# Experts' tiles in pairs while there are two, and the odd last one as a job of its own, in a graph, attention and expert layer on Trainium2

## The chip, the cores and the metric

The kernel runs on one core of a Trainium2 chip. The metric is the device time of one execution in microseconds; less is better. TensorE (PE) multiplies matrices, with its weight loads shown apart (PEld), VectorE (DVE) and ScalarE (ACT) do elementwise work, GpSimd (POOL) issues the indirect transfers, and SyncE (SP) the plain ones of this stage.

## The reference

A layer for 6250 tokens of 256 features and 100000 edges. After a layer norm it adds a graph convolution (mean over the neighbours) and a linear attention; both come before the stage that changes here. Then, on the layer norm of that result, each token goes to one of 8 experts, an MLP of 256 to 1024 to 256 with ReLU:

```python
T = B * L                                           # 6250
C = max(1, math.ceil(CAPACITY_FACTOR * T / E))      # 977
probs = jax.nn.softmax(x @ gate_w + gate_b, axis=-1)
idx = jnp.argmax(probs, axis=-1)
prb = jnp.take_along_axis(probs, idx[:, None], axis=1)[:, 0]
pos = (jnp.cumsum(one_hot, axis=0) * one_hot).sum(-1).astype(jnp.int32) - 1
kept = pos < C
buf = jnp.zeros((E, C, D), dtype=h.dtype).at[idx, pos_safe].set(x, mode='drop')
hmid = jax.nn.relu(jnp.einsum('ecd,edf->ecf', buf, w1) + b1[:, None, :])
ybuf = jnp.einsum('ecf,efd->ecd', hmid, w2) + b2[:, None, :]
y_tok = ybuf[idx, pos_g] * (prb * kept)[:, None]
y = jnp.nan_to_num(y, nan=0.0, posinf=10000.0, neginf=-10000.0)
```

The result is the sum of the layer's input to this stage and y. A token beyond an expert's 977 places gets no expert's output. Everything is in f32.

## The kernel before

The work runs in three stretches. The first normalises the tokens, sorts the edges and prepares the attention. The second, the gather stage, goes over 49 blocks of 128 tokens and multiplies gathered neighbour rows (tile zb) and rows kept in SBUF (z_s) with matrices of counts in add_rows (L821, L822). Beside it, in groups of up to 7 blocks, gate_pieces normalises finished tokens, picks their expert, writes a row of 513 numbers for each (normalised token, residual, probability) to buf_d in device memory, and adds to the tile places, which holds, for each of 64 tiles of 128 places (8 experts, 8 tiles each), which token stands there (L1091). ebase holds the running numbers of tokens of each expert (L1044).

The third stretch, from L1160 on, is the expert stage. It begins with a table worked out on VectorE, replicated over the partitions. From the number of tokens of each expert, capped at CAP = 977, it makes the number of pairs of tiles of each expert (a shift by 8 bits, L1173), their running sum cum (seven additions of one column, L1177), for each of NS = 32 numbers of a pair its expert exp_f and its place among that expert's pairs, and from these the column of places of each of its two tiles. One matmul (L1198) picks these columns out of places, transposed, and its output is cast into idx_s (L1199), the rows of buf_d to gather, and tki_s (L1204), the rows of the output to store. exp_s (L1205, L1206) holds the experts' numbers and the number of pairs, to be read into registers.

Then come the pairs, each 256 places of one expert, whether its second tile holds tokens or not. A pair s goes through four steps:

- fetch(s): SP reads the experts' numbers into registers, four at a time, and loads the expert's weights with expert_weights (L854): w1e and w2e of 1 MB each and two biases, in tiles of three buffers. POOL gathers the pair's two tiles of 128 rows into bt (L1222), four buffers.
- turned(s): four transposes on PE into pB (L1230), and one copy to bT on VectorE (L1232).
- up(s): for each of 8 blocks f of 128 hidden features two matmuls of 256 columns into pu (L1241; three buffers), and an activation with bias and ReLU into hm on ACT (L1242).
- down(s): for each of the two tiles 8 matmuls of 256 columns into pd (L1250; two buffers), then eight VectorE instructions (L1253 to L1263), which add the bias, multiply by the probability, limit what is not finite and add the residual, and an indirect store by POOL (L1264).

The loop runs over S0 = 24 pairs, with fetch three pairs ahead and turned and up one pair ahead of down:

```python
for s in range(S0):
    if s + 3 < S0:
        fetch(s + 3)
    if s + 1 < S0:
        turned(s + 1)
        up(s + 1)
    down(s)
```

Pairs beyond the 24th lie in blocks of rest, under branches on the number of pairs that is read at the end: two, then more, each pair's four steps one behind the other. The order of instructions on each engine is that of a scheduler, which keeps to the data's order; PE runs, as compiled, the transposes of the next pair, the first two matmuls of down of this one, all of up of the next pair, and the remaining fourteen of down of this one. Waits are semaphores, set by the framework for each tile.

Of the kernel before, what the change touches and what calls it, by code (L numbers as in the profile page):

```python
# [7 lines left out]
F32 = mybir.dt.float32  # L8
BF16 = mybir.dt.bfloat16
F32R = mybir.dt.float32r  # L10
I32 = mybir.dt.int32
AF = mybir.ActivationFunctionType
OP = mybir.AluOpType
AX = mybir.AxisListType
ET = mybir.EngineType

P = 128
N = 6250
D = 256
NT = 49  # L20
# [45 lines left out]
NE, F = 8, 1024  # L66
FC = F // P
CAP = 977
ET_ = -(-CAP // P)
SP_ = ET_ // 2  # L70
NS = 32
S0 = 24
EPS = 1e-5
NZ = 19
OWN = 0.4
# [10 lines left out]
def gnn_mix_moe_kernel(ctx: ExitStack, tc: tile.TileContext, x, src, dst, w1t, b1g, w2t, b2g,  # L86
                       kw, kb, vw, vb, gate_w, gate_b, fw1, fb1, fw2, fb2, out):
    nc = tc.nc
# [10 lines left out]
    const = ctx.enter_context(tc.tile_pool(name="const", bufs=1))  # L99
# [16 lines left out]
    lane = const.tile([P, P], F32, name="lane")  # L116
# [13 lines left out]
    cj = const.tile([P, 2], F32, name="cj")  # L130
    for j in range(2):
        nc.vector.tensor_scalar(cj[:, j:j + 1], prow, -float(j), None, op0=OP.add)
    idx_s = const.tile([P, 2 * NS], I32, name="idx_s")
    tki_s = const.tile([P, 2 * NS], I32, name="tki_s")
    exp_s = const.tile([1, NS + 1], I32, name="exp_s")
    eps = const.tile([P, 1], F32, name="eps")
    nc.vector.memset(eps, EPS)

# [16 lines left out]
    bias = const.tile([P, D], F32, name="bias")  # L155
# [20 lines left out]
    with tc.tile_pool(name="early", bufs=1) as ep, tc.tile_pool(name="work", bufs=2) as wp, \  # L176
# [305 lines left out]
        pn, pr, f = None, None, 1.0  # L482
# [42 lines left out]
        for i, (pat, base0) in enumerate((([[1, NB + 1]], 0), ([[0, NB + 1]], SEG // BW))):  # L525
# [7 lines left out]
                                op1=OP.bitwise_or)  # L533
# [181 lines left out]
        for q in range(1, QL + 1):  # L715
# [39 lines left out]
            j = h // 2  # L755
# [405 lines left out]
    with tc.tile_pool(name="table", bufs=1) as tp, tc.tile_pool(name="wgt", bufs=3) as wgt, \  # L1161
# [4 lines left out]
        def row_of(name, n=NE):  # L1166
            return tp.tile([P, n], F32, name=name)

        cnt, cum = row_of("cnt"), row_of("cum")
        nc.vector.tensor_scalar(cnt, ebase[:, NT, :], float(CAP), float(2 * P - 1), op0=OP.min, op1=OP.add)  # L1170
        cni = tp.tile([P, NE], I32, name="cni")
        nc.vector.tensor_copy(cni, cnt)
        nc.vector.tensor_scalar(cni, cni, 8, None, op0=OP.logical_shift_right)  # L1173
        nc.vector.tensor_copy(cum, cni)
        nc.vector.tensor_scalar(cum[:, :1], cum[:, :1], 1.0, None, op0=OP.max)
        for e in range(1, NE):
            nc.vector.tensor_add(cum[:, e:e + 1], cum[:, e:e + 1], cum[:, e - 1:e])  # L1177
        gone = tp.tile([P, NS, NE], F32, name="gone")
        nc.vector.tensor_tensor(gone, cum[:, None, :].to_broadcast([P, NS, NE]),
                                lane[:, :NS, None].to_broadcast([P, NS, NE]), op=OP.is_le)  # L1180
# [5 lines left out]
        nc.vector.scalar_tensor_tensor(col, exp_f, float(SP_), beg, op0=OP.mult, op1=OP.add)  # L1186
        nc.vector.tensor_scalar(col, col, 2.0, None, op0=OP.mult)
        nt = NE * ET_
        pick = tp.tile([P, NS, 2], F32, name="pick")
        nc.vector.tensor_tensor(pick[:nt], col[:nt, :, None].to_broadcast([nt, NS, 2]),  # L1190
                                cj[:nt, None, :].to_broadcast([nt, NS, 2]), op=OP.is_equal)
        plc = tp.tile([P, nt], F32, name="plc")
        nc.vector.scalar_tensor_tensor(plc, places[:, nt:], float(P), places[:, :nt], op0=OP.mult, op1=OP.add)
        pT = pp.tile([P, 2, P], F32, name="pT")
        nc.tensor.transpose(pT[:nt, 0, :], plc, ident)
        plT = tp.tile([P, P], F32, name="plT")
        nc.vector.tensor_copy(plT[:nt], pT[:nt, 0, :])
        nc.tensor.matmul(pT[:, 1, :2 * NS], plT[:nt], pick[:nt].rearrange("p s j -> p (s j)"), start=True, stop=True)  # L1198
        nc.vector.tensor_copy(idx_s, pT[:, 1, :2 * NS])  # L1199
        nc.vector.tensor_scalar(plT[:, :2 * NS], pT[:, 1, :2 * NS], float(P), float(2 * NT * P), op0=OP.is_lt,  # L1200
                                op1=OP.mult)
        nc.vector.scalar_tensor_tensor(plT[:, :2 * NS], pT[:, 1, :2 * NS], -float(P), plT[:, :2 * NS], op0=OP.add,
                                       op1=OP.add)
        nc.vector.tensor_copy(tki_s, plT[:, :2 * NS])  # L1204
        nc.vector.tensor_scalar(exp_s[:, :NS], exp_f[:1, :], float(NE - 1), None, op0=OP.min)  # L1205
        nc.vector.tensor_copy(exp_s[:, NS:], cum[:1, NE - 1:])  # L1206


        bts, bTs, hms, experts = {}, {}, {}, {}

        def fetch(s, n=4):

            if s not in experts:
                _, es = nc.values_load_multi_w_load_instructions(
                    exp_s[0:1, s:s + n], engines=[ET.SP], min_val=0, max_val=NE - 1,
                    skip_runtime_bounds_check_because="the number of an expert")
                experts.update({s + i: e for i, e in enumerate(es)})
            if s:
                weights[s] = expert_weights(wgt, experts[s])
            bts[s] = wp.tile([P, 2, RW], F32, name="bt", bufs=4)  # L1220
            for j in range(2):
                nc.gpsimd.indirect_dma_start(  # L1222
                    out=bts[s][:, j, :], out_offset=None, in_=buf_d,
                    in_offset=bass.IndirectOffsetOnAxis(ap=idx_s[:, 2 * s + j:2 * s + j + 1], axis=0))

        def turned(s):
            pT = pp.tile([P, 2, 2, P], F32, name="pB", bufs=2)
            for j in range(2):
                for c in range(2):
                    nc.tensor.transpose(pT[:, c, j, :], bts[s][:, j, c * P:(c + 1) * P], ident)  # L1230
            bTs[s] = wp.tile([P, 2, 2 * P], F32, name="bT")
            nc.vector.tensor_copy(bTs[s], pT.rearrange("p c j q -> p c (j q)"))  # L1232

        def up(s):
            w1e, _, b1e, _ = weights[s]
            hms[s] = wp.tile([P, FC, 2 * P], F32, name="hm")
            bT = bTs.pop(s)
            for f in range(FC):
                pu = pp.tile([P, 2 * P], F32, name="pu", bufs=3)
                for c in range(2):  # L1240
                    nc.tensor.matmul(pu, w1e[:, c, f * P:(f + 1) * P], bT[:, c, :], start=(c == 0), stop=(c == 1))  # L1241
                nc.scalar.activation(hms[s][:, f, :], pu, AF.Relu, bias=b1e[:, f:f + 1])  # L1242

        def down(s):
            _, w2e, _, b2e = weights.pop(s)
            hm, bt = hms.pop(s), bts.pop(s)
            for j in range(2):
                pd = pp.tile([P, D], F32, name="pd", bufs=2)
                for f in range(FC):
                    nc.tensor.matmul(pd, hm[:, f, j * P:(j + 1) * P], w2e[:, f, :], start=(f == 0), stop=(f == FC - 1))  # L1250

                yt = wp.tile([P, D], F32, name="yt", bufs=3)
                nc.vector.tensor_add(yt, pd, b2e)  # L1253
                nc.vector.tensor_scalar(yt, yt, bt[:, j, RW - 1:RW], None, op0=OP.mult)
                lim = wp.tile([P, D], F32, name="lim", bufs=3)
                low = wp.tile([P, D], F32, name="low")
                ok = wp.tile([P, D], I32, name="ok")
                nc.vector.tensor_scalar(lim, yt, FMAX, 1e4, op0=OP.is_gt, op1=OP.mult)
                nc.vector.tensor_scalar(low, yt, -FMAX, 1e4, op0=OP.is_lt, op1=OP.mult)
                nc.vector.tensor_sub(lim, lim, low)  # L1260
                nc.vector.tensor_scalar(ok, yt, 0.0, 0.0, op0=OP.mult, op1=OP.is_equal)
                nc.vector.copy_predicated(lim, ok, yt)
                nc.vector.tensor_add(lim, lim, bt[:, j, D:2 * D])  # L1263
                st = nc.gpsimd.indirect_dma_start(  # L1264
                    out=out, out_offset=bass.IndirectOffsetOnAxis(ap=tki_s[:, 2 * s + j:2 * s + j + 1], axis=0),
                    in_=lim, in_offset=None, bounds_check=N - 1, oob_is_err=False)
                tc.declare_no_dep(st.ins, group="result", reason="each token has one place")
                tc.add_to_no_dep_group("result", st.ins)

        for s in range(3):  # L1270
            fetch(s)
        turned(0)
        up(0)
        for s in range(S0):
            if s + 3 < S0:
                fetch(s + 3)
            if s + 1 < S0:
                turned(s + 1)
                up(s + 1)
            down(s)  # L1280

        used_s = nc.values_load(exp_s[0:1, NS:], min_val=1, max_val=NS,
                                skip_runtime_bounds_check_because="the number of pairs")

        def rest(s, n):

            with tc.If(used_s > s):
                for i in range(s, s + n):
                    fetch(i, n)
                    turned(i)  # L1290
                    up(i)
                    down(i)
                if s + n < NS:
                    rest(s + n, 2 if n < 4 and s + n + 2 < NS - 2 else NS - s - n)

        rest(S0, 2)


# [36 lines left out]
```

## Time and profile before

| | us |
|---|---|
| median of 3 timed runs | 1396.89 (1394.22 to 1400.62) |
| profiled execution | 1385.61 |
| its span, first to last instruction | 1383.8 |
| PE busy | 1128.7 (82%) |
| VectorE busy | 759.6 (55%) |
| POOL busy | 536.2 (39%) |
| ACT busy | 439.7 (32%) |
| mean granted clock of TensorE | 0.924 |

The page shows one profiled execution, taken by the hardware profiler; its times are in microseconds from the first instruction on, and line numbers are those of the kernel. In a row of a group of instructions the name left of the arrow is what is written, then come what is read, the shapes, the number of instructions after the x, the busy time, the mean duration in ns, and the idle time of the engine just before them with what ended it. A matmul's duration counts the time in the pipeline, so consecutive matmuls overlap, and their spacing is shorter than their duration. The chain of waits follows the work that ended last back from the end, from each step to what released it; its pieces are start, length and work.

In this execution the first up of the expert stage starts at 1027.4 and the last store's instruction at 1377.9.

### The profile page before, as it was taken

The numbers are of one execution on the slowest core, as the hardware profiler recorded it, in microseconds if no ns is written. First come the engines' busy times: TensorE is split into PE (matmuls) and PEld (weight loads), VectorE is DVE, ScalarE is ACT, GpSimd is POOL, SyncE is SP. The second block draws the span as 40 slices with busy tenths as digits, with TensorE's granted clock in tenths as the row PEclk, the third lists the DMA queues.
The fourth block names the chain that finished last, engine by engine and source line by source line (L and its number), as shares of the span: only waits on it lengthen the run. The fifth ranks groups of instructions, "written<-read, shape, count | busy, mean of one in ns | idle before, by whom it ended". The sixth has DMA issues, their size and how long they took to land.

```text
span 1383.8 us, 21039 instructions
## 1 busy us (share of the span) xinstructions
PE 1128.7 (82%) x7471; PEld 1012.2 (73%) x7471; DVE 759.6 (55%) x2197; ACT 439.7 (32%) x960; POOL 536.2 (39%) x586
## 2 busy tenths in 40 slices
PE   0688968637879789879888888888849999999997
PEld 0477757536768779778778778778738888888886
DVE  8999776644644654644654544546523443434434
ACT  0567834302223232233233233233513222232221
POOL 0000002056665565656656656666122222232221
PEclk9999989857999889989889989999969999999999
DMA  8674213256876885966966866867565556566550
GB/s 252 200 237 173 99 48 130 96 184 206 286 223 180 224 255 175 256 224 186 269 210 186 246 195 197 219 211 193 191 233 170 200 200 231 178 215 216 201 189 21
DMA packets 147804, 269.91 MB, mean 195 GB/s; under 512 B 19139, under 2 KB 92557, under 8 KB 147692
## 3 DMA queue, kind: packets, MB, share of 16 engines
q0 software_dynamic: 42048, 134.90, 30.9%
q1 hardware_dynamic: 75431, 105.44, 24.9%
q10 hardware_dynamic: 30213, 28.15, 6.5%
q8 instruction: 61, 1.00, 0.3%
q14 instruction: 51, 0.42, 0.1%
HBM read 217.11 MB, written 52.21 MB: 195 GB/s over the span
## 4 chain that ended last, share of the span: by engine, by line
PE 60%; issue 7%; DMA 4%; DVE 4%; another core or an unknown queue 3%; ACT 1%; POOL 0%; ACTq 0%; SPq 0%; POOLq 0%; DVEq 0%
PE pa L821 14%; PE pa L822 13%; PE pu L1241 12%; PE pd L1250 12%; PE pc L918 6%; DMA buf_d<-row 3%; PE lgr L1006 1%; PE ph L998 1%; ACT cn L921 1%; PE pB L1230 1%; DMA bt<-buf_d,idx_s 1%; DVE on L892 0%; DVE og L898 0%; DMA y<-y_d 0%
## 5 line engine op out<-in xcount | busy, mean ns | idle before, releaser
L908 POOL DMA_INDIRECT zb<-z_d,idx x441 | 425.0, 964 | 265.1 <-issue 97.0
L821 PE MATMUL pa<-z_s,cn 128*128 128x258 f32 x1176 | 346.3, 322 | 12.8 <-issue 12.3
L822 PE MATMUL pa<-z_s,cn 128*128 128x256 f32 x1176 | 316.4, 296 | 10.6 <-issue 10.2
L921 ACT CAST cn<-pc 128x512 fp32r<-128x512 f32 x294 | 171.2, 587 | 437.9 <-PE pc L918 138.3
L821 PEld LDWEIGHTS pa<-z_s,cn 128*128 128x128 f32 x1176 | 241.1, 205 | 16.1 <-issue 15.9
L822 PEld LDWEIGHTS pa<-z_s,cn 128*128 128x128 f32 x1176 | 241.0, 205 | 12.7 <-issue 11.9
L892 DVE TENSOR_TENSOR on<-lane_w,nvl 128x1024 bf16<-128x1024 bf16 x147 | 101.2, 688 | 233.8 <-PE pc L918 109.7
L1242 ACT ACTIVATE hm<-pu,b1e 128x256 f32<-128x256 f32 x192 | 90.9, 473 | 266.0 <-PE pu L1241 235.9
L1250 PE MATMUL pd<-w2e,hm 128*128 128x256 f32 x768 | 173.3, 379 | 0.0
L1241 PE MATMUL pu<-bT,w1e 128*128 128x256 f32 x768 | 172.7, 383 | 0.0
L918 PE MATMUL pc<-od,on 128*128 128x128 bf16 x1176 | 125.5, 232 | 53.9 <-issue 26.0
L1241 PEld LDWEIGHTS pu<-bT,w1e 128*128 128x128 f32 x768 | 145.0, 191 | 26.8 <-issue 7.8
L1250 PEld LDWEIGHTS pd<-w2e,hm 128*128 128x128 f32 x768 | 144.1, 190 | 18.6
L1264 POOL DMA_INDIRECT out_dram<-lim,tki_s x48 | 48.3, 1006 | 254.1 <-DVE lim L1263 245.7
L821 PE MATMUL pa<-zb,og 128*128 128x258 f32 x441 | 130.2, 308 | 9.2 <-issue 8.8
L918 PEld LDWEIGHTS <-on 128*128 128x128 bf16 x1176 | 76.9, 103 | 72.3 <-issue 50.0
L822 PE MATMUL pa<-zb,og 128*128 128x256 f32 x441 | 124.9, 296 | 4.1 <-issue 3.7
L1253 DVE TENSOR_TENSOR yt<-pd,b2e 128x256 f32<-128x256 f32 x48 | 20.4, 425 | 192.7 <-PE pd L1250 192.7
L821 PEld LDWEIGHTS pa<-zb,og 128*128 128x128 f32 x441 | 90.1, 204 | 10.5 <-issue 10.3
L822 PEld LDWEIGHTS pa<-zb,og 128*128 128x128 f32 x441 | 90.1, 204 | 8.0 <-issue 8.0
L587 POOL DMA_INDIRECT kb<-srt_d,bi x5 | 5.2, 1044 | 203.2 <-DVE bi L583 202.0
L419 PE MATMUL pz<-w2s,xTa 128*128 128x256 f32 x196 | 56.8, 412 | 13.7 <-ACT xTa L430 13.1
(382 smaller groups left out, 1497.5 us busy)
## 6 DMA issues: line engine op xcount, KB each, us to landing
w1e<-in_fw_dram SPq DMA_DIRECT2D x24, 1024.0 KB
w2e<-in_fw_dram SPq DMA_DIRECT2D x24, 1024.0 KB
z_d<-zr SPq DMA_DIRECT2D x49, 256.0 KB
buf_d<-row SPq DMA_DIRECT2D x6, 1795.5 KB
zb<-z_d,idx POOLq DMA_INDIRECT x441
ovf_d<-zero ACTq DMA_DIRECT2D x1, 6321.0 KB
ov<-ovf_d SPq DMA_DIRECT2D x49, 129.0 KB
y_d<-xg ACTq DMA_DIRECT2D x7, 896.0 KB
```

The costliest lines, as they stand in the source:

```text
L419: nc.tensor.matmul(pz, xT[:, c, :], w2s[:, c, :], start=(c == 0), stop=(c == 1))
L821: nc.tensor.matmul(ps[:, :AW], lhsT, z[:, D:], start=first, stop=False, skip_group_check=True)
L822: nc.tensor.matmul(ps[:, :D], lhsT, z[:, :D], start=False, stop=last, skip_group_check=True)
L892: nc.vector.tensor_tensor(to[b % 2][:, c, :].rearrange("p c (m j) -> p c m j", j=2), lanes[:, None, :w].to_broadcast([P, n, w, 2]), of.to_ ...
L908: nc.gpsimd.indirect_dma_start(out=zb[asked % NZ].bitcast(F32)[:, :DZ], out_offset=None, in_=z_d, in_offset=bass.IndirectOffsetOnAxis(ap=i ...
L918: nc.tensor.matmul(pc[:, j - j0, :], on[:, j // 2, (j % 2) * P:(j % 2 + 1) * P], od[:, j // 2, :], start=True, stop=True, skip_group_check ...
L921: nc.scalar.copy(cn[:, :n, :], pc[:, :n, :])
L1241: nc.tensor.matmul(pu, w1e[:, c, f * P:(f + 1) * P], bT[:, c, :], start=(c == 0), stop=(c == 1))
L1242: nc.scalar.activation(hms[s][:, f, :], pu, AF.Relu, bias=b1e[:, f:f + 1])
L1250: nc.tensor.matmul(pd, hm[:, f, j * P:(j + 1) * P], w2e[:, f, :], start=(f == 0), stop=(f == FC - 1))
L1253: nc.vector.tensor_add(yt, pd, b2e)
L1264: st = nc.gpsimd.indirect_dma_start(out=out, out_offset=bass.IndirectOffsetOnAxis(ap=tki_s[:, 2 * s + j:2 * s + j + 1], axis=0), in_=lim, ...
```

## The change

An expert's tiles are still taken two at a time while there are two. If their number is odd, the last one is a job of its own, of one tile. The table gets the numbers of tiles by a shift of 7 bits, the pairs by one bit more, odd (whether an expert has an odd tile), and ods_, its running sum; own1, of1, exp1 and col1 give for each of up to 8 odd tiles its expert and its column of places, which go into 8 further columns of pick, idx_s and tki_s and into exp_s. The matmul that picks has 72 columns instead of 64. Three numbers (more) decide at the end whether anything is left.

The loop runs over a list of jobs: S0 = 21 pairs and S1 = 3 odd tiles, the latter behind the 5th, 10th and 15th pair. An odd tile is numbered NS + i; turned, up and down work on as many tiles as tiles_of gives: two transposes, an up of 128 columns, a down of one output. Its weights are loaded as those of a pair. At the end one branch guards two chains of rest blocks, one for further pairs and one for further odd tiles.

```diff
-S0 = 24
+S0 = 21
+S1 = 3
+NC = 2 * NS + NE
...
-        nc.vector.tensor_scalar(cnt, ebase[:, NT, :], float(CAP), float(2 * P - 1), op0=OP.min, op1=OP.add)
+        nc.vector.tensor_scalar(cnt, ebase[:, NT, :], float(CAP), float(P - 1), op0=OP.min, op1=OP.add)
         cni = tp.tile([P, NE], I32, name="cni")
         nc.vector.tensor_copy(cni, cnt)
-        nc.vector.tensor_scalar(cni, cni, 8, None, op0=OP.logical_shift_right)
+        nc.vector.tensor_scalar(cni, cni, 7, None, op0=OP.logical_shift_right)
+        nc.vector.tensor_copy(cnt, cni)
+        nc.vector.tensor_scalar(cni, cni, 1, None, op0=OP.logical_shift_right)
         nc.vector.tensor_copy(cum, cni)
         nc.vector.tensor_scalar(cum[:, :1], cum[:, :1], 1.0, None, op0=OP.max)
+        odd, ods_ = row_of("odd"), row_of("ods_")
+        nc.vector.scalar_tensor_tensor(odd, cum, -2.0, cnt, op0=OP.mult, op1=OP.add)
+        nc.vector.tensor_scalar(odd, odd, 0.0, None, op0=OP.max)
+        nc.vector.memset(ods_[:, :1], 0.0)
         for e in range(1, NE):
             nc.vector.tensor_add(cum[:, e:e + 1], cum[:, e:e + 1], cum[:, e - 1:e])
+            nc.vector.tensor_add(ods_[:, e:e + 1], ods_[:, e - 1:e], odd[:, e - 1:e])
...
+        sing = [P, NE, NE]
+        own1, of1 = (tp.tile(sing, F32, name=n) for n in ("own1", "of1"))
+        nc.vector.tensor_tensor(own1, ods_[:, None, :].to_broadcast(sing),
+                                lane[:, :NE, None].to_broadcast(sing), op=OP.is_equal)
+        nc.vector.tensor_mul(own1, own1, odd[:, None, :].to_broadcast(sing))
+        exp1, col1, of_e = row_of("exp1"), row_of("col1"), row_of("of_e")
+        nc.vector.tensor_mul(of1, own1, lane[:, None, :NE].to_broadcast(sing))
+        nc.vector.tensor_reduce(exp1, of1, AX.X, OP.add)
+        nc.vector.scalar_tensor_tensor(of_e, lane[:, :NE], float(ET_), cnt, op0=OP.mult, op1=OP.add)
+        nc.vector.tensor_scalar(of_e, of_e, -1001.0, None, op0=OP.add)
+        nc.vector.tensor_mul(of1, own1, of_e[:, None, :].to_broadcast(sing))
+        nc.vector.tensor_reduce(col1, of1, AX.X, OP.add)
+        nc.vector.tensor_scalar(col1, col1, 1000.0, None, op0=OP.add)
+        nc.vector.tensor_scalar(pick[:nt, 2 * NS:], col1[:nt], cj[:nt, :1], None, op0=OP.is_equal)
...
-        nc.vector.tensor_copy(exp_s[:, NS:], cum[:1, NE - 1:])
+        nc.vector.tensor_copy(exp_s[:, NS:NS + NE], exp1[:1])
+        nc.vector.tensor_add(ods_[:, NE - 1:], ods_[:, NE - 1:], odd[:, NE - 1:])
+        more = row_of("more", 3)
...
+        nc.vector.tensor_copy(exp_s[:, NS + NE:], more[:1])
...
+        def tiles_of(s):
+            return (2 * s, 2 * s + 1) if s < NS else (NS + s,)
...
         def up(s):
             w1e, _, b1e, _ = weights[s]
+            q = P * len(tiles_of(s))
             hms[s] = wp.tile([P, FC, 2 * P], F32, name="hm")
             bT = bTs.pop(s)
             for f in range(FC):
-                pu = pp.tile([P, 2 * P], F32, name="pu", bufs=3)
+                pu = pp.tile([P, 2 * P], F32, name="pu", bufs=3)[:, :q]
                 for c in range(2):
-                    nc.tensor.matmul(pu, w1e[:, c, f * P:(f + 1) * P], bT[:, c, :], start=(c == 0), stop=(c == 1))
-                nc.scalar.activation(hms[s][:, f, :], pu, AF.Relu, bias=b1e[:, f:f + 1])
+                    nc.tensor.matmul(pu, w1e[:, c, f * P:(f + 1) * P], bT[:, c, :q], start=(c == 0), stop=(c == 1))
+                nc.scalar.activation(hms[s][:, f, :q], pu, AF.Relu, bias=b1e[:, f:f + 1])
...
-            for j in range(2):
+            for j, c in enumerate(tiles_of(s)):
...
+        jobs = list(range(S0))
+        for i in range(S1):
+            jobs.insert((i + 1) * S0 // (S1 + 1) + i, NS + i)
...
+        for i, s in enumerate(jobs):
+            if i + 3 < len(jobs):
+                ask(i + 3)
+            if i + 1 < len(jobs):
+                turned(jobs[i + 1])
+                up(jobs[i + 1])
             down(s)
...
+        with tc.If(counted(0, NS + 1) > 1):
+            rest(counted(1, NS + 1), S0, 2, NS)
+            rest(counted(2, NE + 1), NS + S1, 2, NS + NE)
```

More of the change, by code (lines that the diff above doesn't have):

```diff
@@ L132, in gnn_mix_moe_kernel @@
         nc.vector.tensor_scalar(cj[:, j:j + 1], prow, -float(j), None, op0=OP.add)
-    idx_s = const.tile([P, 2 * NS], I32, name="idx_s")
-    tki_s = const.tile([P, 2 * NS], I32, name="tki_s")
-    exp_s = const.tile([1, NS + 1], I32, name="exp_s")
+    idx_s = const.tile([P, NC], I32, name="idx_s")
+    tki_s = const.tile([P, NC], I32, name="tki_s")
+    exp_s = const.tile([1, NS + NE + 3], I32, name="exp_s")
     eps = const.tile([P, 1], F32, name="eps")
@@ L1188, in gnn_mix_moe_kernel @@
         nt = NE * ET_
-        pick = tp.tile([P, NS, 2], F32, name="pick")
-        nc.vector.tensor_tensor(pick[:nt], col[:nt, :, None].to_broadcast([nt, NS, 2]),
+        pick = tp.tile([P, NC], F32, name="pick")
+        nc.vector.tensor_tensor(pick[:nt, :2 * NS].rearrange("p (s j) -> p s j", j=2),
+                                col[:nt, :, None].to_broadcast([nt, NS, 2]),
                                 cj[:nt, None, :].to_broadcast([nt, NS, 2]), op=OP.is_equal)
+        sing = [P, NE, NE]
[12 more added lines that the diff above has]
+        nc.vector.tensor_scalar(pick[:nt, 2 * NS:], col1[:nt], cj[:nt, :1], None, op0=OP.is_equal)
         plc = tp.tile([P, nt], F32, name="plc")
@@ L1197, in gnn_mix_moe_kernel @@
         nc.vector.tensor_copy(plT[:nt], pT[:nt, 0, :])
-        nc.tensor.matmul(pT[:, 1, :2 * NS], plT[:nt], pick[:nt].rearrange("p s j -> p (s j)"), start=True, stop=True)
-        nc.vector.tensor_copy(idx_s, pT[:, 1, :2 * NS])
-        nc.vector.tensor_scalar(plT[:, :2 * NS], pT[:, 1, :2 * NS], float(P), float(2 * NT * P), op0=OP.is_lt,
+        nc.tensor.matmul(pT[:, 1, :NC], plT[:nt], pick[:nt], start=True, stop=True)
+        nc.vector.tensor_copy(idx_s, pT[:, 1, :NC])
+        nc.vector.tensor_scalar(plT[:, :NC], pT[:, 1, :NC], float(P), float(2 * NT * P), op0=OP.is_lt,
                                 op1=OP.mult)
-        nc.vector.scalar_tensor_tensor(plT[:, :2 * NS], pT[:, 1, :2 * NS], -float(P), plT[:, :2 * NS], op0=OP.add,
+        nc.vector.scalar_tensor_tensor(plT[:, :NC], pT[:, 1, :NC], -float(P), plT[:, :NC], op0=OP.add,
                                        op1=OP.add)
-        nc.vector.tensor_copy(tki_s, plT[:, :2 * NS])
+        nc.vector.tensor_copy(tki_s, plT[:, :NC])
         nc.vector.tensor_scalar(exp_s[:, :NS], exp_f[:1, :], float(NE - 1), None, op0=OP.min)
-        nc.vector.tensor_copy(exp_s[:, NS:], cum[:1, NE - 1:])
+        nc.vector.tensor_copy(exp_s[:, NS:NS + NE], exp1[:1])
+        nc.vector.tensor_add(ods_[:, NE - 1:], ods_[:, NE - 1:], odd[:, NE - 1:])
+        more = row_of("more", 3)
+        nc.vector.tensor_scalar(more[:, 1:2], cum[:, NE - 1:], 1.0, None, op0=OP.add)
+        nc.vector.tensor_scalar(more[:, 2:3], ods_[:, NE - 1:], 1.0, None, op0=OP.add)
+        nc.vector.tensor_scalar(more[:, 0:1], more[:, 1:2], -float(S0), 1.0, op0=OP.add, op1=OP.max)
+        nc.vector.tensor_scalar(odd[:, :1], more[:, 2:3], -float(S1), 1.0, op0=OP.add, op1=OP.max)
+        nc.vector.tensor_tensor(more[:, 0:1], more[:, 0:1], odd[:, :1], op=OP.max)
+        nc.vector.tensor_copy(exp_s[:, NS + NE:], more[:1])
         bts, bTs, hms, experts = {}, {}, {}, {}
+        def tiles_of(s):
+            return (2 * s, 2 * s + 1) if s < NS else (NS + s,)
         def fetch(s, n=4):
@@ L1220, in fetch @@
             bts[s] = wp.tile([P, 2, RW], F32, name="bt", bufs=4)
-            for j in range(2):
+            for j, c in enumerate(tiles_of(s)):
                 nc.gpsimd.indirect_dma_start(
                     out=bts[s][:, j, :], out_offset=None, in_=buf_d,
-                    in_offset=bass.IndirectOffsetOnAxis(ap=idx_s[:, 2 * s + j:2 * s + j + 1], axis=0))
+                    in_offset=bass.IndirectOffsetOnAxis(ap=idx_s[:, c:c + 1], axis=0))
         def turned(s):
+            n = len(tiles_of(s))
             pT = pp.tile([P, 2, 2, P], F32, name="pB", bufs=2)
-            for j in range(2):
+            for j in range(n):
                 for c in range(2):
@@ L1231, in turned @@
             bTs[s] = wp.tile([P, 2, 2 * P], F32, name="bT")
-            nc.vector.tensor_copy(bTs[s], pT.rearrange("p c j q -> p c (j q)"))
+            nc.vector.tensor_copy(bTs[s].rearrange("p c (j q) -> p c j q", j=2)[:, :, :n], pT[:, :, :n])
         def up(s):
             w1e, _, b1e, _ = weights[s]
+            q = P * len(tiles_of(s))
             hms[s] = wp.tile([P, FC, 2 * P], F32, name="hm")
@@ L1246, in down @@
             hm, bt = hms.pop(s), bts.pop(s)
-            for j in range(2):
+            for j, c in enumerate(tiles_of(s)):
                 pd = pp.tile([P, D], F32, name="pd", bufs=2)
@@ L1264, in down @@
                 st = nc.gpsimd.indirect_dma_start(
-                    out=out, out_offset=bass.IndirectOffsetOnAxis(ap=tki_s[:, 2 * s + j:2 * s + j + 1], axis=0),
+                    out=out, out_offset=bass.IndirectOffsetOnAxis(ap=tki_s[:, c:c + 1], axis=0),
                     in_=lim, in_offset=None, bounds_check=N - 1, oob_is_err=False)
@@ L1268, in down, with ask, counted, rest @@
                 tc.add_to_no_dep_group("result", st.ins)
-        for s in range(3):
-            fetch(s)
+        jobs = list(range(S0))
+        for i in range(S1):
+            jobs.insert((i + 1) * S0 // (S1 + 1) + i, NS + i)
+        def ask(i):
+            s = jobs[i]
+            fetch(s, min(4, S0 - s) if s < NS else S1)
+        for i in range(3):
+            ask(i)
         turned(0)
         up(0)
[L1274 to L1279, printed above, removed]
-            down(s)
[L1282 to L1287, printed above, removed]
+        for i, s in enumerate(jobs):
[4 more added lines that the diff above has]
+                up(jobs[i + 1])
+            down(s)
+        def counted(i, hi):
+            return nc.values_load(exp_s[0:1, NS + NE + i:NS + NE + i + 1], min_val=1, max_val=hi,
+                                  skip_runtime_bounds_check_because="a number of tiles")
+        def rest(used, s, n, end):
+            with tc.If(used > (s + 1 if s < NS else s - NS + 1)):
                 for i in range(s, s + n):
-                    fetch(i, n)
+                    fetch(i, s + n - i)
                     turned(i)
@@ L1292, in rest @@
                     down(i)
-                if s + n < NS:
-                    rest(s + n, 2 if n < 4 and s + n + 2 < NS - 2 else NS - s - n)
-        rest(S0, 2)
+                if s + n < end:
+                    rest(used, s + n, 2 if n < 4 and s + n + 2 < end - 2 else end - s - n, end)
+        with tc.If(counted(0, NS + 1) > 1):
+            rest(counted(1, NS + 1), S0, 2, NS)
+            rest(counted(2, NE + 1), NS + S1, 2, NS + NE)
 _IN = [
```

## The prediction

> **What bounds the kernel now.** I read the page's costliest groups first. They say how much of the expert stage was run:
>
> ```profile
> L1250 PE MATMUL pd<-w2e,hm 128*128 128x256 f32 x768 | 173.3, 379 | 0.0
> L1241 PE MATMUL pu<-bT,w1e 128*128 128x256 f32 x768 | 172.7, 383 | 0.0
> ```
>
> One f32 `matmul` call shows as two instructions here. For a pair `up` makes 8 x 2 calls and `down` 2 x 8, so each line has 32 instructions per pair: 768 / 32 = 24 pairs, 48 tiles; no block of `rest` ran, and PE never idled in front of either line (0.0). Next, the busy table by stretch, for everything before the first `up`, the stage, and one pair of it:
>
> ```profile
> core 0: us, PE busy (x) PEld busy (x) DVE busy (x) ACT busy (x) POOL busy (x), PEclk, DMA share, GB/s
> 1004.00:1027.40 23.40, 3.88 (x15) 2.31 (x16) 9.15 (x59) 0.75 (x2) 7.56 (x8) 0.50 0.70 243
> 1027.40:1378.00 350.60, 347.39 (x1627) 299.28 (x1625) 142.99 (x407) 90.88 (x192) 86.62 (x88) 1.00 0.55 185
> 1051.15:1065.60 14.45, 14.45 (x69) 12.46 (x69) 5.96 (x18) 3.79 (x8) 3.97 (x4) 1.00 0.62 208
> ```
>
> In the stage PE is busy throughout at a granted clock of 1.00; DVE, ACT and POOL have over half a pair's 14.45 us free and DMA moves for 62% of it. The chain of waits agrees; one pair is four pieces:
>
> ```profile
> 1049.85 0.44 PE pB L1230 x4
> 1050.28 0.86 PE pd L1250 x4
> 1051.15 7.11 PE pu L1241 x32
> 1058.26 6.04 PE pd L1250 x28
> ```
>
> So a matmul instruction taken off this stage is time off the end, at its spacing and not at its duration (379 ns counts the pipeline): 6.04 / 28 = 0.2157 us.
>
> **How much is taken off.** The reference's inputs, put through its formulas, send 568, 522, 1723, 618, 1040, 1150, 389 and 240 tokens to the eight experts. Capped at 977 that is 5, 5, 8, 5, 8, 8, 4 and 2 tiles of 128: 45, of which pairs alone make 24 (the 48 tiles of the trace, three of them empty). After the change there are 21 pairs and 3 odd tiles, exactly S0 and S1: still 24 jobs and 24 loads of weights, and both lists of `rest` stay untaken.
>
> **One odd tile against one pair.** `down` runs 16 instructions instead of 32, all still 256 wide: 16 x 0.2157 = 3.45 us saved. `turned` runs two transposes instead of four: 0.22 saved. `up` keeps its 32 instructions and 32 weight loads, but streams 128 columns where it streamed 256. The nearest row is the f32 matmul of 128 columns in the first stage, and beside it the gather stage, where each 256-wide one-pass instruction has its own 128x128 f32 weight load:
>
> ```profile
> 102.28 0.61 PE L422 MATMUL pz<-less_mean,xTa 128*128 128x128 f32 x4
> 102.73 0.38 PE L398 MATMUL pT<-ident,xn 128*128 128x128 f32 x2
> ...
> 981.64 0.28 PE L822 MATMUL pa<-z_s,cn 128*128 128x256 f32 x1
> 981.76 0.28 PE L821 MATMUL pa<-z_s,cn 128*128 128x258 f32 x1
> 981.88 0.28 PE L822 MATMUL pa<-z_s,cn 128*128 128x256 f32 x1
> ```
>
> Four of L422 take 102.73 - 102.28 = 0.45, or 0.1125 each, same type and width; L821/L822 show weight loads sustained at one per 0.12. I take 0.1125 and keep 0.12. A pair's 7.11 is 32 x 0.2157 = 6.90 plus 0.21 of start; the odd tile's is 32 x 0.1125 + 0.21 = 3.81, saved 3.30 (3.06 at 0.12; none if the width did not matter at all).
> The Trainium skill (TensorE: Matmul & The Clock Gate, LDWEIGHTS and Back-to-back issue gap) speaks against this term: a load lasts columns / 1.2 ns, 107 ns for 128 columns whatever is streamed, and a stream of load and matmul pairs is spaced by both. As an estimate from that page, a load that was not hidden would make 107 + 107 = 214 ns, no gain in `up`, and the whole sum -10.0; hidden, about 107 ns and -20.5. The rows above, loads of 190 ns each at 0.1125 to 0.12 spacing, speak for hidden.
> Per odd tile 3.45 + 0.22 + 3.30 = 6.97 us; three of them **-20.9 us**.
>
> **What hides the rest.** An odd tile lasts 14.45 - 6.97 = 7.48 us. ACT: eight activations; 473 ns at 256 columns less the 107 by which its copy falls from 373 (128x256) to 266 (106x128) is 366 each, 2.9 us, under the 0.45 that PE takes per block of four; at a full 473 it would set the pace, +0.2 us per odd tile. DVE: one chain of 2.9 busy us (the 141 us of L1253 to L1263 over 48) plus a copy of at most 0.69, which the four `pd` instructions (0.86) ahead of `up` cover as now. POOL: one gather and one store, about 2 us; each queue loses an entry per odd tile and a gather still stands three jobs ahead. SP: the same two 1 MB loads per job. `w1e` of a job is asked for behind `w2e` of the job before, after its `down`, and has two jobs of cover: 28.9 us between pairs, 21.9 with an odd tile, for 2 MB at 185 to 243 GB/s, about 10 us. If the cover failed PE would wait for `w1e`: the second rival. The extra reading of expert numbers on SP (L1214; the issues around one are 0.98 apart, at 1051.12 and 1052.10, those without one 0.54, at 1065.57 and 1066.11: 0.44) is in the same cover.
>
> **What is added: the table.** Counting the instruction order up to the cast into `idx_s`, VectorE gets 29 more small instructions, in front of the first gather, where nothing covers them, since from 1008.8 to 1027.4 PE has only the table's two steps and the first transposes.
>
> ```profile
> 1010.12 0.34 DVE L1177 TENSOR_TENSOR cum<-cum 128x1 f32<-128x1 f32 x2
> 1010.49 0.42 DVE L1179 TENSOR_TENSOR gone<-cum,lane 128x256 f32<-128x256 f32 x1
> 1012.99 0.22 DVE L1190 TENSOR_TENSOR pick<-col,cj 64x64 f32<-64x64 f32 x1
> 1013.26 0.69 PE L1198 MATMUL pT<-pick,plT 64*128 64x64 f32 x2 [3.38 <-DVE pick L1190]
> 1013.98 0.23 DVE L1199 CAST idx_s<-pT 128x64 int32<-128x64 f32 x1 [0.78 <-PE pT L1198]
> 1015.43 0.94 POOL L1222 DMA_INDIRECT bt<-buf_d,idx_s  x1 [38.77 <-DVE tki_s L1204]
> ```
>
> A dependent instruction of this size starts 0.18 to 0.20 after its producer, one that depends on nothing recent 0.08 after its predecessor (L1044 at 1006.06, L1046 at 1006.14, L1170 at 1006.26, L1047 at 1006.34). The first 7 fall between steps of the gate's last piece. The running sum `ods_` alternates with `cum`, so a pair of sums costs about what one did, but only two `cum` sums now precede the copy of `plT`, which waits for PE until 1009.92; five remain behind it where two did: `gone` starts at about 1011.1, +0.6. The instructions on [P, 8, 8] sit between dependent ones of 256 elements (0.46 apart, 0.35 of it streaming), about 0.05 too many each: +0.35 by `pick`. The six on `more` lie in the 0.78 that DVE waits for PE. Together **+1.0 us**. Ends: 0 (all hidden; a gain is excluded, as nothing on this chain is removed) and 29 x 0.2 = 5.8 (none hidden). SP's first read of expert numbers moves by about 1.4 too, but the weights it fetches were wanted only at 1036.7.
> The skill's VectorE: DVE Perf Modes, The DRAIN you can't avoid, has the next instruction wait until the pipe is empty, unless nothing holds it; taken strictly that is 29 x 0.17 = 4.9 as an estimate and -16. The starts 0.08 apart, at durations of 0.16, show the exception here.
> The branch at the end reads one number, as before, and its block is skipped: 0.
>
> **Sum.** -20.9 + 1.0 = -19.9. The profiled execution took 1385.61 (span 1383.8, 1.8 around it): 1365.7, span 1363.9. The three timed runs lie 9 to 15 us above it, median 1396.89; nothing in the stage explains that and I carry it over: **1377.0**.
>
> **Rivals.**
> *`up` does not shrink* (weight loads or ACT set its pace). For: 32 loads of 190 ns remain. Against: 0.1125 at L422. -3 x 3.67 + 1.0 = -10.0: 1387.
> *The weights come late.* For: a pair moves 208 GB/s x 14.45 us = 3.0 MB; an odd tile, less one gather and one store (0.4 MB by their shapes), 2.6 MB in 7.48 us, 350 GB/s. Against: three buffers spread it; two pairs and an odd tile make 8.6 MB in 36.4 us, 236 GB/s, the rate that 1004 to 1027 sustains at 70% of the DMA engines. If each odd tile ends no earlier than its pair did: 1398.
> *A list is too short, slower.* The profile cannot show it, since 48 tiles ran either way. At the 22nd pair (expert 3 would need 641 tokens, has 618) `rest` runs two unpipelined pairs: 2 x 14.45 plus an opening of 12.0 as from 1015.43 to 1027.43, +41: 1418. At a fourth odd tile (expert 6 at 384 tokens, has 389) two odd ones, 2 x 7.48 + 12 = +27: 1404. It decides only if the chip's rounding moves tokens by that many.
>
> **Chances.** Forecast 0.84, the rivals 0.07, 0.05 and 0.04. Within 0.5%, 7.0 us here, is about what a measurement of this kernel cannot tell from no change (1389.9 to 1403.9). Faster: the forecast and nearly all of the first rival, 0.90; same: the second, 0.06; slower: the third, 0.04. Range: the table at 5.8 gives 1382 and the runs' spread is 3 to 4 us each way, so 1387 at the top, which takes in the first rival; below, 0.108 per `up` instruction and no table give 1375.5, less the spread 1371, to 1370.
>
> **What would show it.** Right: `up` in two shapes, 672 instructions of 256 and 96 of 128 columns spaced 0.11 to 0.12, `pd` x720, 45 gathers, a step in the chain of about 7.5 us three times, the first `up` 1.0 us later behind the last sum into `places`, no PE idle in the odd tiles. Wrong: PE waiting for `w1e` around them, 96 narrow instructions at 0.2, the first gather later by several us, or more than 24 jobs.

## The result and the profile after

The changed kernel took 1379.23 us (median of 4 runs, 1377.11 to 1381.49) beside 1395.56 for the kernel before (1392.12 to 1400.62); the ratio of the runs is 0.9854, with a 95% interval of 0.9813 to 0.9894. A second series, of the same kernel, gave 1372.96 beside 1396.75, ratio 0.9848 (0.9813 to 0.9884). The forecast was 1377.0 in a range of 1370 to 1387, 19.9 us faster.

The profiled execution of the changed kernel took 1377.47 us, span 1375.5. Its groups of PE instructions, kept apart by shape (line, shapes, count, then busy us and mean ns), show what was run in the expert stage; L1290 and L1281 are the lines that were L1250 and L1241:

```profile
L1290 PE MATMUL pd<-w2e,hm 128*128 128x256 f32 x720 | 163.0, 379 | 0.0
L1281 PE MATMUL pu<-bT,w1e 128*128 128x256 f32 x672 | 151.8, 384 | 0.0
L1281 PE MATMUL pu<-bT,w1e 128*128 128x128 f32 x96 | 11.3, 276 | 0.0
```

720 / 16 = 45 tiles instead of 48, in 672 / 32 = 21 pairs and 96 / 32 = 3 odd tiles, and no idle time of PE in front of either line. The chain of waits around the first odd tile (start, length, work):

```profile
1106.51 0.22 PE pB L1269 x2
1106.73 0.86 PE pd L1290 x4
1107.59 3.62 PE pu L1281 x32
1111.21 6.05 PE pd L1290 x28
1117.26 0.44 PE pB L1269 x4
1117.70 0.87 PE pd L1290 x4
1118.56 7.11 PE pu L1281 x32
1125.67 2.59 PE pd L1290 x12
```

Two transposes (0.22), `up` in 3.62 where a pair has 7.11, and 4 + 12 instructions of `down` (0.87 + 2.59) where a pair has 4 + 28. An odd tile is 7.30 us of PE and a pair 14.46: 7.16 saved, three times 21.5. At the head, the table and the first gather in the changed kernel's timeline, and the chain up to the first `up`:

```profile
1028.54 0.23 DVE L1224 CAST idx_s<-pT 128x72 int32<-128x72 f32 x1
1029.52 0.94 POOL L1260 DMA_INDIRECT bt<-buf_d,idx_s  x1 [40.26 <-DVE tki_s L1229]
```

```profile
1032.04 7.48 DMA bt<-buf_d,idx_s
1039.56 0.69 PE pB L1269 x2
1040.25 8.66 PE pu L1281 x32
```

All of this lies some 13 us later in the execution than in the profile before, because the stages ahead took longer in this one. So I measure from the last step of ebase, the last work in common, which started at 1006.06 before and at 1019.59 here. From it, in us, for all profiles (the last eight rows are the experiments below; the lower four of them ran in the second set; where the second job is an odd tile, or the chain of waits does not pass the start of the second `up`, that place is blank):

| profile | to the first gather | to the first up | to the second up | to the end of the span |
|---|---|---|---|---|
| before | 9.37 | 21.37 | 30.63 | 377.7 |
| changed | 9.93 | 20.66 | 30.40 | 355.9 |
| changed, again | 9.94 | 21.10 | 30.71 | 356.4 |
| up wide | 9.95 | 20.73 | 30.52 | 365.8 |
| pair in the branch | 9.93 | 20.54 | 30.66 | 385.6 |
| weights later | 9.93 | 17.00 | 26.77 | 352.5 |
| before, again | 9.49 | 20.91 | 30.32 | 377.2 |
| table alone | 10.17 | 20.93 | 31.31 | 378.9 |
| odd ones together | 9.93 | 20.42 | | 355.5 |
| before, weights later | 9.11 | 16.10 | | 373.4 |

The change is worth 377.5 - 356.2 = 21.3 us there (means of two profiles each; 21.5 with the first set's profile of before alone), and nothing of it lies ahead of the second `up`.

### The profile page after: what moved, and what is told of

Same layout as the page of the kernel before. It is cut to its first block, busy times and chain, and to the rows that moved or that the text cites. A ratio compares the mean times of both kernels' runs of the same rounds, so it can differ in the third digit from the quotient of the medians.

```text
span 1375.5 us, 20920 instructions
## 1 busy us (share of the span) xinstructions
PE 1108.2 (81%) x7417; PEld 995.8 (72%) x7417; DVE 751.6 (55%) x2202; ACT 437.6 (32%) x960; POOL 528.9 (38%) x580
## 4 chain that ended last, share of the span: by engine, by line
PE 62%; issue 5%; DVE 5%; DMA 3%; another core or an unknown queue 3%; ACT 1%; POOL 0%; ACTq 0%; DVEq 0%; POOLq 0%
PE pa L823 15%; PE pa L824 13%; PE pu L1281 12%; PE pd L1290 11%; PE pc L920 7%; DMA buf_d<-row 2%; PE lgr L1008 2%; PE ph L1000 1%; ACT cn L923 1%; PE pB L1269 1%; DVE on L894 1%; DMA bt<-buf_d,idx_s 1%; DVE row L974 0%; DVE og L900 0%
## 5 line engine op out<-in xcount | busy, mean ns | idle before, releaser
L823 PE MATMUL pa<-z_s,cn 128*128 128x258 f32 x1176 | 348.8, 324 | 12.4 <-issue 11.8
L1282 ACT ACTIVATE hm<-pu,b1e 128x256 f32<-128x256 f32 (+1 forms) x192 | 88.3, 460 | 246.8 <-PE pu L1281 221.4
L1281 PE MATMUL pu<-bT,w1e 128*128 128x256 f32 (+1 forms) x768 | 163.1, 371 | 0.0
L1290 PE MATMUL pd<-w2e,hm 128*128 128x256 f32 x720 | 163.0, 379 | 0.0
L1281 PEld LDWEIGHTS pu<-bT,w1e 128*128 128x128 f32 x768 | 138.3, 192 | 24.1 <-issue 7.3
L1290 PEld LDWEIGHTS pd<-w2e,hm 128*128 128x128 f32 x720 | 134.8, 190 | 17.2
L1304 POOL DMA_INDIRECT out_dram<-lim,tki_s x45 | 45.3, 1007 | 238.8 <-DVE lim L1303 227.9
```

What stands on the lines that cost most here:

```text
L823: nc.tensor.matmul(ps[:, :AW], lhsT, z[:, D:], start=first, stop=False, skip_group_check=True)
L1282: nc.scalar.activation(hms[s][:, f, :q], pu, AF.Relu, bias=b1e[:, f:f + 1])
L1304: st = nc.gpsimd.indirect_dma_start(out=out, out_offset=bass.IndirectOffsetOnAxis(ap=tki_s[:, c:c + 1], axis=0), in_=lim, in_offset=None, ...
```

## The experiments

The runs were made in two sets, each beside its own runs of the kernel before: 1396.75 us in the first and 1284.74 in the second. The experiments of the two sets ran on different chips, numbered 7 and 15. Times of whole executions are compared within a set; the way from ebase to the end, which took 377.7 us in the one and 377.2 in the other for the kernel before, also across them.

**The changed kernel again** (first set; no edit).

> The changed kernel as it is, in five rounds beside the one before. Theory: the expert stage gives 3 x 7.16 = 21.5 us (an odd tile 7.30 instead of 14.46, from the chain of the changed kernel's profile), the table costs 0.6 up to the first gather, and the stages ahead are the same work: 20 to 22 us faster, ratio 0.985, with the last step of ebase at different times in different executions of either kernel, without a lean to one side. Rival: the gather stage itself has become slower (its last step lies at 1019.6 in the changed profile, at 1006.1 in the one before), so that the medians differ by 8 to 14 us only, ratio 0.990 to 0.994, and the last ebase step lies near 1019 again.

Measured: 1372.96, 23.8 below the 1396.75 beside it; ratio 0.9848 (0.9813 to 0.9884). The last step of ebase lies at 1012.2 here and at 1019.6 in the first profile of the same kernel; in the three other profiles of this set that contain the change's table it lies between 1011.2 and 1015.7. The rival wanted a ratio of 0.990 or more; the interval ends at 0.9884, so a loss of that size falls. A smaller one is not excluded: in both sets the profiles without the change's table reach the end of the gather stage earliest (1006.1, against 1011.2 to 1019.6; 902.0 and 906.2, against 906.9 and 911.4), each a single execution; the timed runs of the table alone, below, leave room for 0.3%. The 16.3 between the first medians and the 23.8 between these bracket the 21.3 of the traces.

**`up` over 256 columns for odd tiles too** (first set).

```diff
-            nc.vector.tensor_copy(bTs[s].rearrange("p c (j q) -> p c j q", j=2)[:, :, :n], pT[:, :, :n])
+            nc.vector.tensor_copy(bTs[s].rearrange("p c (j q) -> p c j q", j=2), pT[:, :, :n].to_broadcast([P, 2, 2, P]))
...
-            q = P * len(tiles_of(s))
+            q = 2 * P
```

> The changed kernel, but up works on 256 columns for an odd tile too, with its 128 places copied twice into bT; down still makes one output. Only the narrow matmuls and narrow activations of three jobs are undone. If the width sets their time: 96 instructions at 0.216 to 0.222 instead of 0.113, 3 x 3.5 = 10.5 us slower than the changed kernel, that is 10 to 11 faster than before. If the weight loads or the activations had set the pace of the odd tiles' up: no change, 0 to 2 us.

Measured: 1385.7, 11.0 below before, ratio 0.9925 (0.9901 to 0.995), 12.7 above the changed kernel; from ebase to the end 365.8, 9.6 more. Its chain around the first odd tile:

```profile
1102.77 0.22 PE pB L1269 x2
1102.98 1.30 PE pd L1290 x6
1104.28 6.91 PE pu L1281 x32
1111.19 5.61 PE pd L1290 x26
```

The 32 instructions of `up` take 6.91 instead of 3.62, 3.29 each time and 9.9 in all. The number of instructions, of weight loads and of activations is the same in both kernels, and an activation is shorter than the four instructions that it follows (0.37 of 0.45 us, and 0.47 of 0.86): the width sets the time. `down` with one output and the two transposes less are the other half of the gain: 11.7 us are left against before from ebase to the end (377.5 - 365.8), 11.0 between the medians.

**A pair that falls to the branch** (first set).

```diff
-S0 = 21
+S0 = 20
```

> The changed kernel with S0 = 20, so that the 21st pair falls to the branch, which works on two pairs (the second an empty one). It prices the third rival. One pair less in the loop, -14.46; in the branch 2 x 14.45 and an opening of about 12 in which PE has nothing: +26 us against the changed kernel, so about 5 slower than before. If the branch fetched under the loop's last work, the opening would be hidden: +14.5 only. If the order in the branch leaves the activations uncovered, up to +35.

Measured: 1405.71, 9.0 above before, ratio 1.0076 (1.0046 to 1.0106), and 32.7 above the changed kernel; from ebase to the end 29.4 more. PE's timeline at the end of the loop and in the branch (what is in brackets is the idle time before, and who ended it):

```profile
1339.71 6.64 PE L1290 MATMUL pd<-w2e,hm 128*128 128x256 f32 x30
1354.53 0.66 PE L1269 MATMUL pB<-ident,bt 128*128 128x128 f32 x2 [8.18 <-DMA bt<-buf_d,idx_s]
...
1359.84 8.41 PE L1281 MATMUL pu<-bT,w1e 128*128 128x256 f32 x32
1368.09 7.07 PE L1290 MATMUL pd<-w2e,hm 128*128 128x256 f32 x32
1375.00 7.07 PE L1281 MATMUL pu<-bT,w1e 128*128 128x256 f32 x32
1381.90 7.07 PE L1290 MATMUL pd<-w2e,hm 128*128 128x256 f32 x32
```

The loop's last matmul ends at 1346.4; the branch's first `up` starts 13.5 later, and its four pieces end at 1389.0: 42.6 us of branch for the 14.46 of a pair in the loop. Expected were 26 us against the changed kernel, and 29.4 came: the opening took 13.5 instead of 12, and most of the rest of the difference is not explained. The third rival's mechanism and its price (+41) were real; its condition was not met, as 21 and 3 are exactly what the inputs need.

**The weights of the second and third job asked for later** (first set). In the changed kernel fetch starts with the gathers (moved as they are, not printed here), and the experts' numbers are written behind the first pair's:

```diff
-        nc.vector.tensor_scalar(exp_s[:, :NS], exp_f[:1, :], float(NE - 1), None, op0=OP.min)
+        nc.vector.tensor_scalar(exp_f[:1, :], exp_f[:1, :], float(NE - 1), None, op0=OP.min)
...
+            if not s:
+                nc.vector.scalar_tensor_tensor(exp_s[:, :NS], bts[0][:1, 1, :NS], 0.0, exp_f[:1, :], op0=OP.mult, op1=OP.add)
             if s not in experts:
```

> The changed kernel, but the experts' numbers are written only when the first pair's two gathers have landed (an addition of 0 times the gathered tile), so the weights of the second and third job are asked for behind these gathers. Theory: the first gathers land 4 to 10 us after their issue because some 4 MB of weights are asked for 2 us before them; without that they land in 3 to 4 us, the first up starts 4 to 6 us earlier, and the weights still arrive under the 8 us of the first up: 3 to 6 us faster than the changed kernel. Rival: the landing time is the gather's own, and nothing changes at the first up, or the second up waits for its w1e and the gain is lost: 0, or up to 5 slower.

Measured: 1370.61, ratio to before 0.982 (0.9786 to 0.9854). The intervals of this and of the changed kernel overlap, so the timed runs alone do not separate them. The traces do:

```profile
1023.60 3.82 DMA bt<-buf_d,idx_s
1027.46 0.69 PE pB L1271 x2
1028.15 8.69 PE pu L1283 x32
1036.84 0.22 PE pB L1271 x2
1037.06 0.87 PE pd L1292 x4
1037.92 7.27 PE pu L1283 x32
```

The third gather lands 3.82 us after its issue instead of 7.48, the first `up` starts 7.07 us after the first gather instead of 10.5 to 11.2, and the second `up` takes 7.27 instead of 7.11. Counted from ebase, the first `up` starts 3.7 to 4.1 us earlier than in the changed kernel's two profiles; 4 to 6 were expected. From ebase to the end 352.5: 3.7 less than the changed kernel, and the shortest way of all versions here. The medians lie 26.1 us apart.

**The kernel before again** (second set; no edit).

> The kernel before, unchanged, for a second profile. Theory: the stages ahead of the expert stage take a different time in each execution, and the first profile was a short one: its last step of ebase lay at 1006.1, that of four executions with the change between 1011.2 and 1019.6, and the timed runs of before lie 5 to 17 us above it. So here it lies between 1012 and 1020, the span 6 to 14 us longer, and from that step to the second up 30.6 us as in the first. Rival: the change itself makes the stages ahead slower by 5 to 13 us: then it lies near 1006 again, and the timed runs need another reason.

Measured: 1284.35 beside 1284.74, ratio 0.9997 (0.9974 to 1.0021), the last step of ebase at 902.0. Both expectations of that place failed, since the whole set is 112 us faster than the first: the time went out of the stages ahead, the gather stage above all, with the same program. So this run cannot tell whether the change makes these stages slower. What was said of the way from there to the second `up` held (30.32). The two profiles differ in what VectorE's and ACT's work in the gather stage waited for and in the transfers; the busy table of each, of the instructions that touch the gathered rows zb:

```profile
300.00:900.00 600.00, 144.74 (x744) 116.61 (x744) 368.29 (x382) 0.89 0.74 220
```

```profile
300.00:850.00 550.00, 154.16 (x820) 120.87 (x821) 394.19 (x411) 0.95 0.86 256
```

The last two columns are the share of time in which the DMA engines moved data, and the GB/s: 0.74 and 220 in the first set, 0.86 and 256 in the second. The sets ran on different chips, which is the nearest suspect, but no run here separates the chip from other differences between the sets, so the cause is open.

**The table alone** (second set). The list of odd tiles is worked out and stays empty:

```diff
-S0 = 21
-S1 = 3
+S0 = 24
+S1 = 0
...
-        nc.vector.tensor_scalar(cni, cni, 1, None, op0=OP.logical_shift_right)
+        prs = row_of("prs")
+        nc.vector.tensor_scalar(prs, ebase[:, NT, :], float(CAP), float(2 * P - 1), op0=OP.min, op1=OP.add)
+        nc.vector.tensor_copy(cni, prs)
+        nc.vector.tensor_scalar(cni, cni, 8, None, op0=OP.logical_shift_right)
```

> The kernel with the change's table but no odd tiles: the pairs are counted as before (24 in the loop, two more small instructions for that), the odd list is worked out and stays empty. It prices the 29 added VectorE instructions alone. As recorded: +1.0 us at the first up. From the changed kernel's profiles: 0.56 to 0.6 later from the last step of ebase to the first gather (9.4 to 9.9 or 10.0), and 0.8 to 1.4 given back because the gathers land sooner, so 0 within 0.5 at the second up. In the timed runs the same as before within 0.3%.

Measured: 1288.08, 3.3 above the median beside it, ratio of the runs 1.0006 (0.9983 to 1.0029). First gather 10.17 after ebase against 9.37 and 9.49 without the table, first `up` 20.93 against 21.37 and 20.91, second `up` 31.31 against 30.63 and 30.32. So +0.7 at the gather, nothing at the first `up`, and +0.8 at the second, outside the half microsecond that I had allowed. The +0.8 comes from the clock inside the first `up`. The busy table over the first `up` of this run, and then of before in the same set, each divided where the clock changes (the column before the last two is the granted clock):

```profile
932.29:936.99 4.70, 4.70 (x13) 3.66 (x12) 0.00 (x0) 0.95 (x2) 0.00 (x0) 0.50 1.03 384
936.99:941.58 4.59, 4.59 (x23) 4.00 (x23) 0.00 (x0) 2.37 (x5) 0.00 (x0) 1.00 0.55 171
```

```profile
922.92:925.66 2.74, 2.74 (x7) 2.15 (x7) 0.00 (x0) 0.47 (x1) 0.00 (x0) 0.50 1.04 379
925.66:931.25 5.59, 5.59 (x28) 4.87 (x27) 0.00 (x0) 2.84 (x6) 0.00 (x0) 1.00 0.57 181
```

Both start within 0.02 us of each other, counted from ebase. Here the first 4.70 us ran at 0.50 and the first `up` lasted 9.29 us; there it was 2.74, and 8.33. In the first profile of before it was 2.45, and 8.18; in those of the changed kernel 3.42 and 3.15, and 8.66 and 8.53. In all nine profiles whose first two jobs are pairs the first `up` lasts 6.95 us plus half of what it spent at 0.50. What differs is when the clock comes back, and the clock records of these traces show a grid for that: in all ten profiles every stretch at either clock, but for the first and last of a trace, lasts a multiple of 3.413 us. Where the first `up` falls on that grid changes from execution to execution. So the +0.8 of this profile cannot be put down to the table.

**The odd tiles one behind the other** (second set).

```diff
-            jobs.insert((i + 1) * S0 // (S1 + 1) + i, NS + i)
+            jobs.insert(1 + i, NS + i)
```

> The changed kernel with the three odd tiles one behind the other, right behind the first pair, instead of behind the 5th, 10th and 15th. It tests the cover of the weights: three jobs of 7.3 us ask 2.6 MB each, 356 GB/s, above the 349 that 98% busy DMA engines moved while the first gathers landed. Theory: the three buffers still carry it, since the pairs that follow give the time back; PE waits for no weights: within 2 us of the changed kernel. Rival: w1e or w2e of the odd tiles or of the pair behind them is late, and PE waits 3 to 8 us there.

Measured: 1259.2, 25.5 below the 1284.74 beside it, ratio 0.98 (0.977 to 0.983); from ebase to the end 355.5. The chain through the last two odd tiles and the pair behind them:

```profile
953.43 0.22 PE pB L1269 x2
953.65 0.87 PE pd L1290 x4
954.52 3.62 PE pu L1281 x32
958.14 2.59 PE pd L1290 x12
960.73 0.44 PE pB L1269 x4
961.17 0.87 PE pd L1290 x4
962.03 7.11 PE pu L1281 x32
969.14 2.59 PE pd L1290 x12
```

Not a gap: three jobs of 7.3 us in a row, and PE waits for no weights. From ebase to the end it is within a microsecond of the changed kernel (355.9 and 356.4, in the first set; it did not run in the second). Working on the odd tiles in between is not what saves the time.

**The kernel before, with the weights later** (second set). The same edit of fetch and exp_s, without odd tiles.

> The kernel before with only the weights of the second and third pair asked for behind the first pair's gathers, as in the run that did so on the changed kernel, which gained 4.1 us between gather and first up there. Theory: the same 4 to 5 us here, so that it has nothing to do with odd tiles; 3 to 5 us faster than before, the landing of the third gather 4 us instead of 8.75. Rival: the second pair's weights are a pair's here too and come no later, so no other outcome is expected unless the second up waits: then 0 to 2.

Measured: 1280.65, ratio 0.9969 (0.9945 to 0.9993); from ebase to the end 373.4 against 377.2 and 377.7. The first `up` starts 6.99 after the first gather, against 11.42 and 12.00. So the landing of the first gathers is a cost of both kernels, and it has nothing to do with the odd tiles. The gain is 4.1 us between the medians, 3 to 5 expected. About 0.6 us was given back in the second `up`: its activations waited for their bias b1e, which is asked for behind the 2 MB of that pair's weights and landed 12.07 us after it was asked for.

## Why the prediction was right

*Counts.* 45 tiles, 24 jobs, branch untaken, as worked out from the inputs.

*The stage, -20.9.* It gave -21.5. `down` and the transposes came out as said (3.45 and 0.22). The term that was mis-sized is `up`: 3.49 saved instead of 3.30. The spacing of 0.1125 taken from L422 holds over 32 in a row (3.62 / 32 = 0.113). What I had added, the 0.21 of a pair's start, is for the most part not paid by an odd tile. The timeline of the changed kernel shows why, the copy to bT and PE's work beside it for a pair and then for the first odd tile:

```profile
1092.53 0.69 DVE L1271 COPY bT<-pB 128x512 f32<-128x512 f32 x1
1092.33 1.03 PE L1290 MATMUL pd<-w2e,hm 128*128 128x256 f32 x4
1093.32 0.45 PE L1281 MATMUL pu<-bT,w1e 128*128 128x256 f32 x1
```

```profile
1106.89 0.41 DVE L1271 COPY bT<-pB 128x256 f32<-128x256 f32 x1
1106.57 1.03 PE L1290 MATMUL pd<-w2e,hm 128*128 128x256 f32 x4
1107.43 0.32 PE L1281 MATMUL pu<-bT,w1e 128*128 128x128 f32 x1
```

A pair's `up` starts 0.99 after the covering `pd` instructions began, 0.10 after its copy has ended (1093.22); an odd tile's starts 0.86 after, which is the four instructions' own spacing, and its copy had ended 0.13 before. So a pair waits 0.13 us for its copy, an odd tile does not: the prediction's "cover as now" was not a full cover. The rule weighed there, the Trainium skill's on the time of a weight load (TensorE: Matmul & The Clock Gate, LDWEIGHTS), gives 107 ns for a load of 128 columns, and the measurement differs for f32: each of these 32 loads takes 190 ns in the trace. They start 0.112 apart like the matmuls and overlap, so the estimate for a load that is not hidden, 214 ns per pair of load and matmul, did not come. Whether the streaming (half of 0.2157 is 0.108) or the loads set the 0.112 is not shown by these runs.

*The table, +1.0.* Up to the cast into idx_s it is what was worked out: 7.92 us from ebase before, 8.95 in the changed kernel's second profile (gone +0.67, pick +0.88, the cast +1.03). The step that failed is the one that carried this to the first `up` unchanged: it came 20.5 to 21.1 us behind ebase in the first set's profiles with the weights not moved, not 1.0 behind the 21.4 and 20.9 of before. The first gather starts only 0.5 later, because POOL started it 1.2 to 1.6 us behind the cast in the three profiles without the table and 1.0 behind it in all seven with it; why is open. The third gather then lands 7.2 to 7.9 us after its issue instead of 8.2 and 8.75. SP asks for the weights 2.0 us (in one run 1.3) ahead of the first gather instead of 2.8 to 2.9, and the two runs with these weights moved behind the gathers show that they are what the landing waits for; that the shorter lead is what made it land sooner fits, but was not tested by itself. At the second `up` the four changed profiles of the first set whose weights were not moved lie at 30.4 to 30.7 and the two of before at 30.3 and 30.6: no cost that can be seen. The 31.3 of the table's own run is its longer time at half clock. That leaves a cost of the table of up to some 0.5 us neither shown nor excluded.

*The cover.* ACT's activation on 128 columns took 368 ns, estimated at 366. The DMA rate was put a little low: over two pairs and an odd tile (36.2 us of the second profile) the engines moved 251 GB/s against my 236, at 75% of the time; in the 21.8 us next to the odd tile it was 80 to 86% of the time, 277 and 280 GB/s. It did not bind, nor with three odd tiles in a row.

*The rivals.* That `up` would not shrink was refuted by the wide version; that weights come late by the odd ones together. The branch has its price, 42.6 us, and was not entered.

*The median.* I carried the difference to the timed runs over unchanged. 1379.23 instead of 1377.0 in the first series and 1372.96 in the second lie on either side, as far apart as executions of this kernel do. That the first lies within 2.2 is partly luck: the end of the gather stage lies anywhere from 1006.1 to 1019.6 in the first set's profiles, and for that reason the sum's time for the profiled execution, 1365.7, was missed by 11.8 (1377.47), though the expert stage gained what was forecast. And the gain of 21.3 where 19.9 was forecast is two terms that were both too careful: 0.6 from `up`, 1.0 from the table.

## What to carry to other kernels

Where PE is busy without a gap, work padded away is time gained at the instructions' spacing. Instructions left out pay at that spacing (`down`); streaming 128 columns instead of 256 brought that spacing from 0.216 to 0.112 us here, with the weight loads hidden; fewer columns were not tried. A static number of jobs that fits the data exactly is worth its branch only while it fits: one pair more in an unpipelined branch cost more than the whole gain (29.4 us against 21.3). Price a longer head not to the instruction that it delays but to the next point where PE runs at full clock, expect a microsecond there from when the clock comes back, and look at what the queue beside it asks for meanwhile.

## What the runs showed of the hardware that was not expected

- Two 1 MB loads for each of two jobs, asked for by SP from 1.3 to 2.9 us ahead of small gathers on, made the third gather land after 7.2 to 8.75 us; asked for behind them, after 3.8. While the gathers landed the DMA engines moved data for 98% of the time at 349 GB/s in the changed kernel's second profile, and for 77% at 199 with the weights later.
- After the wait for the gathers PE ran the first 2.45 to 4.70 us of the first `up` at a granted clock of 0.50, and each microsecond at 0.50 cost half of one; the clock's changes lie on a grid of 3.413 us whose place against the first `up` differs between executions of the same kernel. The Trainium skill (TensorE: Matmul & The Clock Gate, Part 1: The HAM clock gate) has the clock come back after about 3.4 us of activity, in a window that runs freely; the multiples of 3.413 us in all ten traces agree with that.
- The same program took 1396.75 us on one chip and 1284.74 on another, the difference all ahead of the expert stage, with the DMA engines moving 220 and 256 GB/s in the gather stage; the cause is open. The expert stage took the same time in both.
